# Reordering the statistics, the table terms and the raw products ahead of the first affine step of a pairwise outer-product batch norm

## The chip, the cores and the metric

The kernel runs on one core of a Trainium2 chip. The engines are called as in the profile: PE (matmuls), DVE (vector engine), ACT (scalar engine), POOL (GpSimd) and SP, which issues the stores; the DMA engines move the bytes, and a stretch is called dry where they have little or nothing to move. The metric is the device time of one execution in microseconds (us).

## The reference

```python
cross  = xj[:, rows, :, None] * xi[:, cols, None, :]   # 1024 x 741 x 16 x 16, pairs col < row of 39 fields
mean   = mean(cross, axis=(0, 2, 3)); var = mean((cross - mean)**2, axis=(0, 2, 3))   # one per pair
normed = (cross - mean) * rsqrt(var + 1e-5) * gamma + beta
out    = transpose(normed[:, :, None] * W)             # 777 MB of float32
```

The inputs are 5 MB, the output 777 MB. The mean and the variance of a pair need only sums over the inputs: means and second moments of each field and their products, summed over the batch (a Gram matrix). So the kernel can know scale and shift of every pair before it forms a product, except for the raw products that it forms meanwhile, to have something to do.

## The kernel before

`xi_sb` and `xj_sb` hold the inputs, 128 partitions by 8 slices. The output is cut into tiles of one row of pairs and two slices; `y_sb` has room for four such tiles, and the statistics borrow the place of tiles 2 and 3 in it as scratch. Instructions keep the order of the program on each engine. g1 is the copy of the first Gram product's sums; k, q1 and q2 are terms of the pairs' means and variances (the variance needs q1 less the square of k); "the table" holds scale and shift of every pair. A raw product is one that is not scaled yet; an affine step scales and shifts it. The parts that matter here, shortened ("..." and comments stand for what is left out):

```python
def product(n, engine, t, i, src):          # one of 16 outer-product rows of one slice of tile n
    ...                                      # ACT: activation(Copy, scale=xj);  POOL: tensor_scalar

def affine(n):                               # tiles 0 and 1: scale and shift of raw products, column by column
    for c in range(r):
        if c % 2 == 0: nc.scalar.activation(y[:, :, c], y[:, :, c], Identity, bias=t_c, scale=s_c)   # L194
        else:          nc.gpsimd.tensor_scalar(y[:, :, c], y[:, :, c], s_c, t_c, mult, add)           # L196

def products(n):                             # tiles 2, 3, ...: products of an xi that is scaled already
    split = E - (POOL_I_LONG if tiles[n][0] > TWO else POOL_I)     # rows below split on ACT, 4 of 16 on POOL
    ...
def finish(n):   # DVE (13% of the columns POOL): add the shift, times W, column by column (L238); store the pieces
    ...

# statistics, n = 0..7: xj side for even n, xi side for odd n
for n in range(7): deviation(n)              # POOL, L283
emit(raw0, 3)                                # raw products of tile 0 on ACT
for n in range(8):
    square(n)                                # ACT, L293
    emit(raw0, 2)
    moments(n)                               # DVE, L299
    if n == 0: deviation(7)
    if n % 2 == 1: gram(n // 2 * T)          # PE, L316: 3 products per slice
    if n in (1, 3): sums(n + 3, n + 5); means(n + 3); means(n + 4)      # DVE
emit(raw_products(1, nc.gpsimd, range(8, 32)), 24)      # raw products of tile 1 on POOL
nc.scalar.copy(w_dve, w_sb)
emit(raw0, 8)
nc.scalar.copy(g1, ps_g[0]);  nc.scalar.copy(e_aa, ps_g[1])
emit(raw0, 5)
# table terms, DVE: k, q2, k, q2, p_q1, p_q2, q1, p_mean ... then
nc.scalar.activation(p_kk, k, AF.Square)     # ACT, "the Square"
# DVE: q1, q1 + p_q2, q1 - p_kk, max/eps, reciprocal
nc.scalar.activation(rstd, inv, AF.Sqrt)     # ACT, "the Sqrt"
emit(raw1, 8)                                # raw products of tile 1 on ACT
# DVE: one Newton step, PE: spread over partitions, DVE: table in st_sb
apply(0); affine(0); weigh(0)                # weigh: DVE, times W (L204), and the stores, piece by piece
scale_xi(2); affine(1); weigh(1); apply(2); apply(1)
# then for each tile n: finish(n), products(n + 1)
```

## Time and profile before

| | before |
|---|---|
| median | 1891.21 us (3 runs, 1891.14 to 1891.22) |
| written | 776.99 MB |
| first store | 41.27 us |
| DVE begins tile 2 | 63.96 us |

Lines of the page for groups of instructions give: line, engine, operation, out and in, count, then busy us and mean ns, then the engine's idle time ahead of them and who ended it. These are the affine steps of tiles 0 and 1 in the kernel before:

```profile
L194 ACT ACTIVATE y_sb<-y_sb,st_sb 128x512 f32<-128x512 f32 x20 | 14.2, 797 | 0.0
L196 POOL TENSOR_SCALAR y_sb<-y_sb,st_sb 128x512 f32<-128x512 f32 x18 | 13.5, 771 | 0.3 <-issue 0.3
```

ACT does not idle ahead of them, POOL only 0.3 us. The view in order of time (start and duration in us, then the same columns) shows what fills the place ahead on DVE and POOL:

```profile
23.83 5.52 DVE L299 TENSOR_REDUCE y_sb<-y_sb 128x78 f32<-128x1248 f32 x4
25.86 11.87 POOL L141 TENSOR_SCALAR y_sb<-xi_sb,xj_sb 128x304 f32<-128x304 f32 x24
```

DVE reduces the last moments until 29.35 us. POOL forms its 24 raw products until 37.73, just as the table is ready (37.90).

### The profile page before, as it was taken

The numbers are of one execution on the slowest core, as the hardware profiler recorded it, in microseconds if no ns is written. First come the engines' busy times: TensorE is split into PE (matmuls) and PEld (weight loads), VectorE is DVE, ScalarE is ACT, GpSimd is POOL, SyncE is SP. The second block draws the span as 40 slices with busy tenths as digits, with TensorE's granted clock in tenths as the row PEclk, the third lists the DMA queues.
The fourth block names the chain that finished last, engine by engine and source line by source line (L and its number), as shares of the span: only waits on it lengthen the run. The fifth ranks groups of instructions, "written<-read, shape, count | busy, mean of one in ns | idle before, by whom it ended". The sixth has DMA issues, their size and how long they took to land. (4 is left out here: it accounts for less than half of the span.)

```text
span 1889.3 us, 10288 instructions
## 1 busy us (share of the span) xinstructions
PE 24.5 (1%) x128; PEld 23.1 (1%) x128; DVE 1730.7 (92%) x2612; ACT 1621.3 (86%) x3625; POOL 1574.5 (83%) x1985
## 2 busy tenths in 40 slices
PE   3100000000000000000000000000000000000000
PEld 3100000000000000000000000000000000000000
DVE  7999999998989898989898989899999999999996
ACT  8999989898989898989898989888888888888762
POOL 9798878788888888888888888888888888888972
DMA  4999999999999999999999999999999999999999
GB/s 164 390 418 429 425 427 429 430 424 429 424 425 426 424 424 426 422 425 425 424 425 423 426 423 426 422 422 422 421 421 422 418 415 419 416 419 419 415 419 390
DMA packets 70288, 783.67 MB, mean 415 GB/s; under 512 B 5057, under 2 KB 6209, under 8 KB 15937
## 3 DMA queue, kind: packets, MB, share of 16 engines
q1 hardware_dynamic: 69632, 780.46, 98.3%
q10 hardware_dynamic: 576, 2.56, 0.3%
q14 instruction: 79, 0.64, 0.1%
q8 instruction: 1, 0.02, 0.0%
HBM read 6.00 MB, written 776.99 MB: 414 GB/s over the span
## 5 line engine op out<-in xcount | busy, mean ns | idle before, releaser
L238 DVE SCALAR_TENSOR_TENSOR y_sb<-y_sb,st_sb,w_dve 128x512 f32<-128x512 f32 x2542 | 1678.5, 740 | 131.5 <-issue 128.3
L139 ACT ACTIVATE y_sb<-xs,xj_sb 128x256 f32<-128x256 f32 (+32 forms) x3544 | 1576.4, 539 | 223.5 <-DMA out_dram<-y_sb 171.8
L141 POOL TENSOR_SCALAR y_sb<-xs,xj_sb 128x560 f32<-128x560 f32 (+35 forms) x1256 | 643.2, 536 | 35.1 <-DMA out_dram<-y_sb 32.6
L230 POOL TENSOR_TENSOR y_sb<-y_sb,w_sb 128x1024 f32<-128x1024 f32 (+4 forms) x138 | 442.0, 3203 | 11.5
L159 POOL TENSOR_TENSOR xs<-xi_sb,st_sb 128x576 f32<-128x576 f32 (+37 forms) x150 | 187.8, 1252 | 225.3 <-ACT y_sb L139 217.8
L226 POOL TENSOR_SCALAR y_sb<-y_sb,st_sb 128x512 f32<-128x512 f32 x384 | 259.4, 692 | 12.9 <-ACT y_sb L139 12.9
L204 DVE TENSOR_TENSOR y_sb<-y_sb,w_dve 128x2560 f32<-128x2560 f32 (+5 forms) x8 | 21.0, 2682 | 2.3 <-ACT y_sb L194 2.3
L139 ACT ACTIVATE y_sb<-xi_sb,xj_sb 128x304 f32<-128x304 f32 x40 | 18.7, 534 | 0.1
L414 PE MATMUL ps<-y_sb 39*128 39x38 f32 (+37 forms) x76 | 16.5, 397 | 5.6 <-DVE y_sb L402 5.6
L414 PEld LDWEIGHTS ps<-y_sb 39*128 39x128 f32 x76 | 16.3, 329 | 5.8 <-issue 5.8
L194 ACT ACTIVATE y_sb<-y_sb,st_sb 128x512 f32<-128x512 f32 x20 | 14.2, 797 | 0.0
L196 POOL TENSOR_SCALAR y_sb<-y_sb,st_sb 128x512 f32<-128x512 f32 x18 | 13.5, 771 | 0.3 <-issue 0.3
L141 POOL TENSOR_SCALAR y_sb<-xi_sb,xj_sb 128x304 f32<-128x304 f32 x24 | 11.9, 518 | 0.0
L299 DVE TENSOR_REDUCE y_sb<-y_sb 128x78 f32<-128x1248 f32 x8 | 11.1, 1442 | 0.0
L277 DVE TENSOR_REDUCE y_sb<-xj_sb 128x78 f32<-128x1248 f32 (+1 forms) x5 | 5.9, 1189 | 5.6 <-DMA xj_sb<-in_r_xj_dram 5.6
L293 ACT ACTIVATE y_sb<-y_sb 128x1248 f32<-128x1248 f32 x8 | 9.9, 1243 | 1.3 <-POOL y_sb L283 1.1
L283 POOL TENSOR_TENSOR y_sb<-xj_sb,y_sb 128x1248 f32<-128x1248 f32 x4 | 9.3, 2314 | 1.9 <-ACT y_sb L327 1.9
L283 POOL TENSOR_TENSOR y_sb<-xi_sb,y_sb 128x1248 f32<-128x1248 f32 x4 | 9.3, 2318 | 0.0
L316 PE MATMUL ps<-y_sb 128*39 128x79 f32 x48 | 7.2, 339 | 16.5 <-DVE y_sb L299 16.5
L316 PEld LDWEIGHTS ps<-y_sb 128*39 128x39 f32 x48 | 6.1, 183 | 17.4 <-DVE y_sb L299 9.6
L277 DVE TENSOR_REDUCE y_sb<-xi_sb 128x78 f32<-128x1248 f32 (+1 forms) x5 | 5.9, 1186 | 0.0
L259 POOL TENSOR_SCALAR_AFFINE_SELECT y_sb<-y_sb 39x4992 f32<-39x4992 f32 x1 | 4.6, 4623 | 0.0
(45 smaller groups left out, 16.9 us busy)
## 6 DMA issues: line engine op xcount, KB each, us to landing
out_dram<-y_sb SPq DMA_DIRECT2D x32, 3072.0 KB, 13.7
out_dram<-y_sb SPq DMA_DIRECT2D x28, 2816.0 KB, 15.7
out_dram<-y_sb SPq DMA_DIRECT2D x32, 1664.0 KB, 14.2
out_dram<-y_sb SPq DMA_DIRECT2D x16, 3328.0 KB, 17.2
out_dram<-y_sb SPq DMA_DIRECT2D x30, 1536.0 KB, 15.2
out_dram<-y_sb SPq DMA_DIRECT2D x12, 3840.0 KB, 17.6
out_dram<-y_sb SPq DMA_DIRECT2D x12, 3584.0 KB, 18.1
out_dram<-y_sb SPq DMA_DIRECT2D x22, 1792.0 KB, 17.4
```

The source lines that it names most:

```text
L139: nc.scalar.activation(y, src, AF.Copy, scale=scale)
L141: engine.tensor_scalar(y, src, scale, 1.0, ALU.mult, ALU.mult)
L159: nc.gpsimd.tensor_tensor(xs, xi_sb[:, t0 : t0 + T, 0:r, :], s_sb[:, :, n0 : n0 + r, :].to_broadcast([P, T, r, E]), ALU.mult,)
L194: nc.scalar.activation(y[:, :, c, :], y[:, :, c, :], AF.Identity, bias=t_c, scale=s_c)
L196: nc.gpsimd.tensor_scalar(y[:, :, c, :], y[:, :, c, :], s_c, t_c, ALU.mult, ALU.add)
L204: nc.vector.tensor_tensor(y[:, :, c0:c1, :], y[:, :, c0:c1, :], w_dve.unsqueeze(1).to_broadcast([P, T, c1 - c0, EE]), ALU.mult,)
L226: nc.gpsimd.tensor_scalar(y[:, :, c, :], y[:, :, c, :], t_sb[:, n0 + c : n0 + c + 1], 1.0, ALU.add, ALU.mult)
L230: nc.gpsimd.tensor_tensor(y[:, :, split:r, :], y[:, :, split:r, :], w_sb.unsqueeze(1).to_broadcast([P, T, r - split, EE]), ALU.mult,)
L238: stt(y[:, :, c, :], y[:, :, c, :], t_sb[:, n0 + c : n0 + c + 1], w_dve.to_broadcast([P, T, EE]), ALU.add, ALU.mult,)
L283: nc.gpsimd.tensor_tensor(devs[n % 7], sources[x][:, t0 : t0 + T], shift[:, x : x + 1, :].unsqueeze(3).to_broadcast([P, T, F, E]), ALU.sub ...
L316: nc.tensor.matmul(acc[0:F, 0 : 2 * F + 1], lhs, fb[:, t], start=t == 0, stop=t == NT - 1)
L414: nc.tensor.matmul(ps[:, :, first[r] - n0 : first[r] - n0 + r], pick[:, r, :], stq[:, :, 0:r], start=True, stop=True,)
```

## The change

The statistics take the xi side of each pair of slices first, so that two of the three Gram products can be done while the xj side is still being squared; the last four slices' sums are taken in one batch; g1 is copied as soon as its products are done, and DVE works out the terms of the table that need only g1 beside the last products; four raw products on ACT and six on POOL move from ahead of the first affine step to behind it. The intent is an earlier table and an earlier first store. The diff is shortened:

```diff
 def step_of(n):
-    t0, x = n // 2 * T, n % 2
+    return n // 2 * T, 1 - n % 2                  # xi side first
...
-    for acc, lhs in zip(ps_g, (fa[:, t, 0:F], fa[:, t, F:2*F], ones[:, 0:F])):
+    terms = ((0, fa[:, t, 0:F]), (2, ones[:, 0:F])) if x else ((1, fa[:, t, F:2*F]),)
+    for acc, lhs in terms:
...
-            if n % 2 == 1: gram(n // 2 * T)
-            if n in (1, 3): sums(n + 3, n + 5); means(n + 3); means(n + 4)
+            gram(n)
+            if n == 1: sums(4, 8); means(4, 8)
-        emit(raw_products(1, nc.gpsimd, range(8, 32)), 24)
+        raw1_pool = raw_products(1, nc.gpsimd, range(8, 32))
+        emit(raw1_pool, 18)
         nc.scalar.copy(w_dve, w_sb)
-        emit(raw0, 8)
         nc.scalar.copy(g1, ps_g[0][0:F, 0 : 2 * F + 1])
+        emit(raw0, 3)
         nc.scalar.copy(e_aa, ps_g[1][0:F, 2 * F : 2 * F + 1])
-        emit(raw0, 5)
+        emit(raw0, 10)
...      # DVE: terms of g1 alone first; now q1 - p_kk stands ahead of p_q2 and of q1 + p_q2
         nc.scalar.activation(p_kk, k, AF.Square)
...
         nc.scalar.activation(rstd, inv, AF.Sqrt)
-        emit(raw1, 8)
+        emit(raw1, 4)
...
         apply(0); affine(0)
+        emit(raw1, 4)
+        emit(raw1_pool, 6)
         weigh(0); scale_xi(2); affine(1)
```

More of the change, by code (lines that the diff above doesn't have):

```diff
@@ L279, in sums, with step_of @@
                 )
+        def step_of(n):
+            return n // 2 * T, 1 - n % 2
         def deviation(n):
-            t0, x = n // 2 * T, n % 2
+            t0, x = step_of(n)
             nc.gpsimd.tensor_tensor(
@@ L290, in square, with means, gram @@
         def square(n):
-            scale = 0.25 / NB**0.5 if n % 2 else 0.25
+            _, x = step_of(n)
+            scale = 0.25 / NB**0.5 if x else 0.25
             nc.scalar.activation(devs[n % 7], devs[n % 7], AF.Square, scale=scale)
         def moments(n):
-            t0, x = n // 2 * T, n % 2
+            t0, x = step_of(n)
             to = fb if x else fa
-            at = slice(F, 2 * F)
-            nc.vector.tensor_reduce(to[:, t0 : t0 + T, at], devs[n % 7], AX.X, ALU.add)
-        def means(n):
-            t0, x = n // 2 * T, n % 2
-            to = fb if x else fa
-            stt(
-                to[:, t0 : t0 + T, 0:F],
-                total[:, t0 : t0 + T, part(x)],
-                1.0 / (E * NB) if x else 1.0 / E,
-                ps_u[:, x : x + 1, :].to_broadcast([P, T, F]),
-                ALU.mult,
-                ALU.subtract,
-            )
-        def gram(t0):
+            nc.vector.tensor_reduce(
+                to[:, t0 : t0 + T, F : 2 * F], devs[n % 7], AX.X, ALU.add
+            )
+        def means(t0, t1):
+            for x, to in enumerate((fa, fb)):
+                stt(
+                    to[:, t0:t1, 0:F],
+                    total[:, t0:t1, part(x)],
+                    1.0 / (E * NB) if x else 1.0 / E,
+                    ps_u[:, x : x + 1, :].to_broadcast([P, t1 - t0, F]),
+                    ALU.mult,
+                    ALU.subtract,
+                )
+        def gram(n):
+            t0, x = step_of(n)
             for t in range(t0, t0 + T):
-                for acc, lhs in zip(ps_g, (fa[:, t, 0:F], fa[:, t, F : 2 * F], ones[:, 0:F])):
+                terms = ((0, fa[:, t, 0:F]), (2, ones[:, 0:F])) if x else ((1, fa[:, t, F : 2 * F]),)
+                for acc, lhs in terms:
                     nc.tensor.matmul(
-                        acc[0:F, 0 : 2 * F + 1], lhs, fb[:, t], start=t == 0, stop=t == NT - 1
+                        ps_g[acc][0:F, 0 : 2 * F + 1], lhs, fb[:, t], start=t == 0, stop=t == NT - 1
                     )
@@ L343, in tile_pair_outer_batchnorm @@
         sums(1, 2)
-        means(0)
-        means(1)
+        means(0, 2)
         sums(2, 4)
-        means(2)
-        means(3)
+        means(2, 4)
         for n in range(7):
@@ L355, in tile_pair_outer_batchnorm @@
             moments(n)
+            gram(n)
             if n == 0:
                 deviation(7)
-            if n % 2 == 1:
-                gram(n // 2 * T)
-            if n in (1, 3):
-                sums(n + 3, n + 5)
-                means(n + 3)
-                means(n + 4)
-        emit(raw_products(1, nc.gpsimd, range(8, 32)), 24)
+            if n == 1:
+                sums(4, 8)
+                means(4, 8)
+        raw1_pool = raw_products(1, nc.gpsimd, range(8, 32))
+        emit(raw1_pool, 18)
         nc.scalar.copy(w_dve, w_sb)
-        emit(raw0, 8)
         nc.scalar.copy(g1, ps_g[0][0:F, 0 : 2 * F + 1])
+        emit(raw0, 3)
         nc.scalar.copy(e_aa, ps_g[1][0:F, 2 * F : 2 * F + 1])
-        emit(raw0, 5)
+        emit(raw0, 10)
         e_ab, e_abb, e_a = g1[:, 0:F], g1[:, F : 2 * F], g1[:, 2 * F : 2 * F + 1]
@@ L380, in tile_pair_outer_batchnorm @@
         stt(k, p_b, u, e_ab, ALU.mult, ALU.add)
-        stt(q2, e_ab, u, p_aab, ALU.mult, ALU.add)
+        stt(p_q1, p_bb, u, e_abb, ALU.mult, ALU.add)
         stt(k, p_v, e_a, k, ALU.mult, ALU.add)
-        stt(q2, p_v_half, e_aa, q2, ALU.mult, ALU.add)
-        stt(p_q1, p_bb, u, e_abb, ALU.mult, ALU.add)
-        stt(p_q2, q2, 2.0, p_v, ALU.mult, ALU.mult)
         nc.vector.tensor_add(q1, p_q1, e_abb)
@@ L388, in tile_pair_outer_batchnorm @@
         nc.scalar.activation(p_kk, k, AF.Square)
+        stt(q2, e_ab, u, p_aab, ALU.mult, ALU.add)
         stt(q1, q1, u, p_aabb, ALU.mult, ALU.add)
+        stt(q2, p_v_half, e_aa, q2, ALU.mult, ALU.add)
+        nc.vector.tensor_sub(q1, q1, p_kk)
+        stt(p_q2, q2, 2.0, p_v, ALU.mult, ALU.mult)
         nc.vector.tensor_add(q1, q1, p_q2)
-        nc.vector.tensor_sub(q1, q1, p_kk)
         nc.vector.tensor_scalar(p_var, q1, 0.0, BN_EPS, ALU.max, ALU.add)
```

## The prediction

> **What bounds the kernel now.** I read the page's head, slices and queues first, then the first 85 us in order of time, then the stretches around the first stores.
>
> ```profile
> PE 24.5 (1%) x128; PEld 23.1 (1%) x128; DVE 1730.7 (92%) x2612; ACT 1621.3 (86%) x3625; POOL 1574.5 (83%) x1985
> DMA  4999999999999999999999999999999999999999
> ...
> q1 hardware_dynamic: 69632, 780.46, 98.3%
> ```
>
> No compute engine is the bound over the whole span. The store queue is busy for 98.3% of it and moves 777 MB that the change leaves alone. So the end is "the last moment at which the DMA engines run dry" plus a constant time for the bytes still to come. I looked for that moment in stretches of half a microsecond: DMA share is 0.00 from 70.5 to 72.0 us and 0.07 in 81.5 to 82.0; in every 50 us stretch from 80 us on it is 0.99 to 1.01. So what counts is when the stores at 66.84, 71.31 and 81.31 us (tiles 2 and 3) can be issued, not when the first store leaves. The start in order of time (start, duration, engine, line, what, idle before it):
>
> ```profile
> 28.25 3.61 ACT L139 ACTIVATE y_sb<-xi_sb,xj_sb 128x304 f32<-128x304 f32 x8
> 29.41 1.80 PE L316 MATMUL ps<-y_sb 128*39 128x79 f32 x12 [0.92 <-DVE y_sb L299]
> 31.77 0.20 ACT L372 COPY y_sb<-ps 39x79 f32<-39x79 f32 x1
> 31.92 2.30 ACT L139 ACTIVATE y_sb<-xi_sb,xj_sb 128x304 f32<-128x304 f32 x5
> 32.34 0.24 DVE L382 SCALAR_TENSOR_TENSOR y_sb<-ps,y_sb 39x39 f32<-39x39 f32 x1
> 34.12 0.19 ACT L388 ACTIVATE ps<-y_sb 39x39 f32<-39x39 f32 x1
> 34.35 0.19 DVE L391 TENSOR_TENSOR y_sb<-y_sb,ps 39x39 f32<-39x39 f32 x1 [0.18 <-ACT ps L388]
> 35.23 0.24 ACT L396 ACTIVATE y_sb<-y_sb 39x39 f32<-39x39 f32 x1 [0.91 <-DVE y_sb L395]
> 37.73 0.17 DVE L427 TENSOR_TENSOR st_sb<-ps,st_sb 128x19 f32<-128x19 f32 x1
> 38.06 6.75 POOL L196 TENSOR_SCALAR y_sb<-y_sb,st_sb 128x512 f32<-128x512 f32 x9 [0.34 <-issue]
> 39.13 14.20 ACT L194 ACTIVATE y_sb<-y_sb,st_sb 128x512 f32<-128x512 f32 x20
> 53.23 27.05 ACT L139 ACTIVATE y_sb<-xs,xj_sb 128x304 f32<-128x304 f32 x61
> 63.96 16.55 DVE L238 SCALAR_TENSOR_TENSOR y_sb<-y_sb,st_sb,w_dve 128x512 f32<-128x512 f32 x25 [1.44 <-ACT y_sb L139]
> ```
>
> The reader is to see **ACT as the path of the prologue**: from 28.25 to 63.9 us it idles only 0.91 us (before the Sqrt). It does raw products, the g1 copy, more raw products, the Square of k, the Sqrt, raw products of tile 1, 20 affine steps of tiles 0 and 1 (14.1 us), then 24 products of tile 2 (24 x 0.444 = 10.7 us). DVE waits for the last of them at 63.96 and is then busy without a break to 125 us, so every store from 66.84 on hangs on that moment. L382 finishes k at 32.58, but its Square starts only at 34.12: ACT was still in its five raw products.
>
> **What the Trainium skill says.** "PSUM — Partial Sum Buffer", section "Engine vs sequencer instructions", says the ScalarE, VectorE and GpSimdE queues are strict FIFO. The trace agrees: the late Square just described. "ScalarE: Activation LUTs", section "What ACT_TABLE_LOAD costs", gives 186 ns + 0.833 ns per element, 93 ns more for a pointer operand, and 93 ns overlap; for 304 elements that is 532 ns, 439 from start to start. The trace has 534 and 441. "VectorE: DVE Perf Modes", section "Mode 1× (REGULAR) — the baseline", has one result per cycle; the reduces of 624 and 1248 elements start 0.73 and 1.365 us apart here, about 1.02 ns per element plus 0.09. "HBM Reference", section "Specifications (TRN2)", has a core alone at about 425 GB/s; stretches from 80 us on show 415 to 431, so the store stream has no room left.
>
> **The change, part by part.**
>
> *Statistics on DVE.* DVE has no gap from 9.21 to 29.35, so it sets when the moments end. Two pairs of sums over two slices (4 x 1.365 = 5.46) become two reduces of 2496 elements: with the slope above, an estimate of 2.64 each, 5.28. Four mean steps (0.145 apart, 0.58) become two of 156 columns, an estimate of 0.22 each, 0.44. Saved: 6.04 - 5.72 = 0.3 us. The last moment starts at about 27.6 instead of 27.92, the seventh at 26.25, ending at 27.7. The deviations on POOL (8 x 2.28 us from 7.63, done at 25.87) keep their pace: only the order within pairs turns.
>
> *Matmuls.* The last group shrinks from 12 PE instructions (1.80 us) to 4. PE starts 0.133 apart and one takes 0.338, so an estimate of 0.74: PE ends near 29.8, not 31.21. The sums behind g1 are complete earlier still, after the sixth of eight instructions of the group before: 27.75 + 5 x 0.133 + 0.338 = 28.75.
>
> *ACT before the Square.* Eight raw products used to fill ACT while PE finished. Now g1 comes straight after the copy of w, at 28.25, so ACT stands still until PE is through: 28.8 to 29.1, about 0.65 us lost. Behind it come 3 + 10 raw products where it was 8 + 5: the same 13, still all ahead of the Square. So the Square moves from 34.12 to about 34.8, although k itself is ready some 2 us earlier than before.
>
> *Table terms on DVE.* The terms that the change brings forward end in a wait for that Square: the subtraction now stands before the product for q2 and the addition, which had run during the wait and now run after it. Two instructions at 0.22 us: 0.45 more. So the Sqrt goes from 35.23 to 35.23 + 0.65 + 0.45 = 36.35, and the first table entries (last step 37.73, end 37.90) to about 39.0.
>
> *Affine of tile 0.* ACT used to be held to 39.13 by its eight raw products of tile 1; with four it is free near 38.5 and waits for the table: start about 39.1, no gain. POOL, whose 24 raw products ended at 37.73 and which started at 38.06, now stands idle from 25.87 + 18 x 0.494 = 34.8 to about 39.2. The first store leaves at 41.3 to 41.5, against 41.27.
>
> *The work put behind it.* Four raw products on ACT (4 x 0.441 = 1.76 us) and six on POOL (6 x 0.494 = 2.96) now stand between the affine steps of tiles 0 and 1, and tile 1's affine steps need them all. ACT gets there at 39.1 + 7.05 + 1.76 = 47.9; POOL only at 39.2 + 6.72 + 2.96 = 48.9, and ACT waits for it. Before, ACT started tile 1's affine at 39.13 + 7.05 = 46.18. The shift is 48.95 - 46.18 = 2.77 us. It passes on whole: 10 affine steps, then 24 products, no slack on ACT, so DVE starts tile 2 at about 66.7. POOL's own affine of tile 1 starts near 50.1 (before: 45.99) and ends near 56.9; weighing tile 1 ends near 63.1 instead of 61.18, and 1.4 us of table steps follow. Both lie ahead of 66.7, so neither binds.
>
> **Sum:** 1891.21 + 2.77 = 1893.98, say 1894.0 us.
>
> **Rivals.**
> - *The table comes earlier, as intended, and time falls by 1 to 3 us.* For it: PE ends 1.4 us earlier, POOL has a hole, ACT has four fewer instructions ahead. Against it: the Square's place in ACT's queue. If ACT got to it when k is ready (about 30.2), the Sqrt could be near 32 and affine of tile 0 near 35, giving 1888 to 1890.
> - *Stores hide it.* If what counts were the first store, the time would stay at 1891.2 to 1891.4. For it: the DMA share after 82 us is 1.00. Against it: the dry stretch at 70.5 to 72 wipes out whatever was gained or lost ahead of it.
> - *Only ACT's own work counts*, POOL's six products being ready in time or ACT's g1 wait being shorter: the shift would be 39.1 + 7.05 + 1.76 - 46.18 = 1.7, so 1892.9.
> - *A second wait:* weighing tile 1 on DVE runs over into tile 2 and adds to the shift. It would need 2 us more than I count; 1895 to 1896.
>
> **Range and chances.** All terms are fractions of a microsecond taken from rows of one trace, and three runs before lie within 0.08 us. The main risk is a step of the chain that I misjudge, not scatter. The third rival and some spare give the low end, 1892.2; the fourth and a slower table the high end, 1895.4. I leave one chance in ten for the first two rivals. A change of 2% would be 38 us, as long as the whole time to the first store, so "same" is all but certain.
>
> **What would show it.** Right: the g1 copy at 28.8 to 29.1 with a wait for PE; the Square still behind ten raw products near 34.8, with DVE idle some 3 to 4 us before the subtraction; the Sqrt near 36.3; POOL idle about 4 us before its first affine step near 39.2; ACT idle about 1 us before tile 1's affine, released by POOL; DVE's first step of tile 2 near 66.7; the dry stretch of the DMA moved by the same 2.8 us; the same 0.99 to 1.01 after it. Wrong: a Square near 31 us, an affine of tile 0 before 38 us, or DVE starting tile 2 before 64.5 us while the end moves otherwise.

## More of the kernel before

The view by stretches has, for each stretch of time, the busy us of PE, its weight loads, DVE, ACT and POOL, with counts, then the clock, the share of the DMA engines' time that is busy, and GB/s:

```profile
70.00:72.00 2.00, 0.00 (x0) 0.00 (x0) 2.00 (x4) 2.00 (x6) 2.00 (x6) 1.00 0.16 64
80.00:82.00 2.00, 0.00 (x0) 0.00 (x0) 2.00 (x4) 2.00 (x6) 2.00 (x5) 1.00 0.80 332
100.00:120.00 20.00, 0.00 (x0) 0.00 (x0) 20.00 (x32) 20.00 (x46) 18.42 (x26) 1.00 1.01 420
140.00:142.00 2.00, 0.00 (x0) 0.00 (x0) 1.97 (x6) 2.00 (x5) 1.92 (x3) 1.00 0.75 313
```

The DMA engines are full from about 42 us on, but for dry stretches near 71 and 82 us and short dips such as that at 141.

## The result

The changed kernel takes 1893.85 us (median of 6 runs, 1893.34 to 1894.34), against 1891.22 us for the kernel before (6 runs, 1890.88 to 1891.45). The ratio is 1.0014, 95% interval 1.0001 to 1.0027. By the 2% measure the two are the same; the change costs 2.6 us.

The page of the changed kernel, the affine groups and the store queue (its profile is of the slowest of the six runs, 1894.34 us, so what it shows is about 0.5 us more than a median run has):

```profile
L196 POOL TENSOR_SCALAR y_sb<-y_sb,st_sb 128x512 f32<-128x512 f32 x18 | 13.5, 767 | 4.8 <-ACT y_sb L139 4.8
L194 ACT ACTIVATE y_sb<-y_sb,st_sb 128x512 f32<-128x512 f32 x20 | 14.3, 800 | 1.4 <-POOL y_sb L141 0.9
q1 hardware_dynamic: 69632, 780.46, 98.1%
```

The busy times are as before; what is new is idle time: 4.8 us on POOL, 1.4 us on ACT. The releaser named for POOL's 4.8 us is an ACT raw product that was done at 38.8; what came just ahead of the start was the last table step of DVE (39.05 to 39.22). In order of time:

```profile
28.18 2.11 PE L323 MATMUL ps<-y_sb 128*39 128x79 f32 x12 [0.61 <-DVE y_sb L303]
29.23 0.22 ACT L375 COPY y_sb<-ps 39x79 f32<-39x79 f32 x1 [1.11 <-PE ps L323]
30.71 4.50 ACT L139 ACTIVATE y_sb<-xi_sb,xj_sb 128x304 f32<-128x304 f32 x10
35.11 0.19 ACT L389 ACTIVATE ps<-y_sb 39x39 f32<-39x39 f32 x1
35.34 0.19 DVE L393 TENSOR_TENSOR y_sb<-y_sb,ps 39x39 f32<-39x39 f32 x1 [3.90 <-ACT ps L389]
36.55 0.24 ACT L400 ACTIVATE y_sb<-y_sb 39x39 f32<-39x39 f32 x1 [1.25 <-DVE y_sb L399]
39.30 7.17 ACT L194 ACTIVATE y_sb<-y_sb,st_sb 128x512 f32<-128x512 f32 x10 [0.51 <-ACT y_sb L139]
46.11 2.98 POOL L141 TENSOR_SCALAR y_sb<-xi_sb,xj_sb 128x304 f32<-128x304 f32 x6
49.13 7.16 ACT L194 ACTIVATE y_sb<-y_sb,st_sb 128x512 f32<-128x512 f32 x10 [0.91 <-POOL y_sb L141]
66.93 3.38 DVE L238 SCALAR_TENSOR_TENSOR y_sb<-y_sb,st_sb,w_dve 128x512 f32<-128x512 f32 x5 [2.60 <-ACT y_sb L139]
```

ACT waits 1.11 us for PE. Then ten raw products stand ahead of the Square, for which DVE waits 3.90 us. ACT waits 1.25 us for the reciprocal, 0.51 us for the table, and 0.91 us for POOL's six late products. In sum ACT idles 3.78 us between 28 and 67 us, against 0.91 us before; the difference, 2.87, is all but the 2.97 us by which DVE begins tile 2 later (66.93 against 63.96). The first store leaves at 41.46, only 0.19 us later. The dry stretches have moved and grown:

```profile
68.00:70.00 2.00, 0.00 (x0) 0.00 (x0) 2.00 (x4) 2.00 (x6) 1.92 (x4) 1.00 0.42 172
74.00:76.00 2.00, 0.00 (x0) 0.00 (x0) 2.00 (x4) 2.00 (x6) 1.95 (x4) 1.00 0.44 183
84.00:86.00 2.00, 0.00 (x0) 0.00 (x0) 2.00 (x4) 2.00 (x6) 2.00 (x5) 1.00 0.78 323
```

The last one stands at 84.5 instead of 81.5 us, 3 us later. The bytes written up to 80 us, summed from the stretches, are 13.1 MB instead of 14.3 MB, and this gap of 1.2 MB, which is 2.9 us at 420 GB/s, is still there at 600 us.

### The profile page after: what moved, and what is told of

It reads as the page before. It is cut to its first block, busy times and chain, and to the rows that moved or that the text cites. A ratio compares the mean times of both kernels' runs of the same rounds, so it can differ in the third digit from the quotient of the medians.

```text
span 1892.6 us, 10284 instructions
## 1 busy us (share of the span) xinstructions
PE 25.4 (1%) x128; PEld 22.8 (1%) x128; DVE 1730.5 (91%) x2608; ACT 1621.6 (86%) x3625; POOL 1574.5 (83%) x1985
## 5 line engine op out<-in xcount | busy, mean ns | idle before, releaser
L194 ACT ACTIVATE y_sb<-y_sb,st_sb 128x512 f32<-128x512 f32 x20 | 14.3, 800 | 1.4 <-POOL y_sb L141 0.9
L277 DVE TENSOR_REDUCE y_sb<-xj_sb 128x39 f32<-128x624 f32 (+2 forms) x4 | 5.8, 1454 | 6.1 <-DMA xj_sb<-in_r_xj_dram 6.1
L277 DVE TENSOR_REDUCE y_sb<-xi_sb 128x39 f32<-128x624 f32 (+2 forms) x4 | 5.8, 1443 | 0.0
## 6 DMA issues: line engine op xcount, KB each, us to landing
out_dram<-y_sb SPq DMA_DIRECT2D x32, 1664.0 KB, 14.3
```

Source lines behind the costliest of these rows:

```text
L194: nc.scalar.activation(y[:, :, c, :], y[:, :, c, :], AF.Identity, bias=t_c, scale=s_c)
```

## The experiments

Each kernel ran five times, in rounds with the kernel before on the same chip, whose median was 1891.15 to 1891.29 in all of them. All gave correct results. The changed kernel itself was not run again in these rounds; its row is from the result above. The table has for each what the theories are about: when DVE begins tile 2 and when the first store leaves (in the profiled run), and the median.

| run | DVE begins tile 2 | first store | median (range) |
|---|---|---|---|
| before | 63.96 | 41.27 | 1891.22 |
| changed | 66.93 | 41.46 | 1893.85 (1893.34 to 1894.34) |
| a_pool_back | 65.56 | 40.91 | 1893.23 (1892.94 to 1893.35) |
| b_g1_filled | 65.76 | 40.29 | 1893.07 (1892.86 to 1893.27) |
| h_terms_back | 66.39 | 40.93 | 1893.61 (1893.33 to 1893.78) |
| d_early_square | 65.12 | 39.64 | 1892.38 (1892.32 to 1892.48) |
| c_early_table | 64.12 | 39.45 | 1891.48 (1891.10 to 1891.74) |
| e_late_store | 63.74 | 44.06 | 1891.26 (1890.79 to 1891.38) |
| g_pool_share | 62.37 | 41.20 | 1889.70 (1889.57 to 1889.87) |
| k_order_share | 60.68 | 37.34 | 1888.13 (1887.87 to 1888.40) |
| f_fine_pieces | 63.88 | 41.20 | 1890.96 (1890.76 to 1891.06) |
| j_fine_all | 63.81 | 41.13 | 1891.12 (1890.97 to 1891.25) |
| l_combined | 60.60 | 37.26 | 1888.03 (1887.91 to 1888.44) |
| m_cut_on | 60.77 | 37.43 | 1888.20 (1887.92 to 1888.35) |

The theory: the time moves one for one with the moment at which DVE begins tile 2, which ACT sets. The rivals: the first store sets it; the early table is worth having for itself; the store stream's dry stretches set it. Over the first ten rows the median moves by 5.7 us and the DVE column by 6.25 us, in the same order but for two pairs that lie 0.2 us apart (a and b, e and before). The first store does not order them: d and c send it 1.6 and 1.8 us earlier than before and are not faster than before, e sends it 2.8 us later and is not slower.

The medians and the profiled runs are not the same executions. For the profiled runs alone, the time less the DVE column lies between 1827.05 and 1827.68 us in all fourteen rows. The traces show how the moment is carried on: in each of them DVE works for 197.9 us from its first step of tile 2 without a wait (198.3 in j and l, with one wait of 0.3), up to about 260 us. Just ahead of that ACT waits 4.5 to 4.6 us for a store to land, and only this wait reaches DVE, which then stands about 4 us.

### a_pool_back: the six POOL products back in front

```diff
-emit(raw1_pool, 18)
+emit(raw1_pool, 24)
 ...
-emit(raw1_pool, 6)
```

> The changed kernel with all 24 raw products of tile 1 on POOL put back ahead of the first affine step; the four on ACT stay behind it. My theory (the path runs through the affine steps of tile 1, which ACT may begin only when POOL's six late products are done): POOL does the six in its 4.8 us hole, ACT begins the affine of tile 1 near 48.2 instead of 49.13 with no wait for POOL, DVE begins tile 2 near 66.0 instead of 66.93, time down by 0.9 us against the changed kernel, to about 1892.9. Rival (only ACT's own count of work and the late table matter; POOL's part is hidden): time unchanged at 1893.8.

Measured: 1893.23 us. The second half of the affine steps no longer waits for POOL:

```profile
38.74 7.16 ACT L194 ACTIVATE y_sb<-y_sb,st_sb 128x512 f32<-128x512 f32 x10 [0.51 <-ACT y_sb L139]
47.75 7.16 ACT L194 ACTIVATE y_sb<-y_sb,st_sb 128x512 f32<-128x512 f32 x10
```

From the first to the second line it is 9.01 us instead of 9.83 in the changed kernel, so 0.82 us of the expected 0.9 came from POOL's products. The rest of the 1.37 us in the DVE column was there from the start: g1 came at 28.67 instead of 29.23 in this profile, with the same program up to there, because the loads had landed sooner.

### b_g1_filled: ACT works while PE finishes

```diff
 nc.scalar.copy(w_dve, w_sb)
+emit(raw0, 8)
 nc.scalar.copy(g1, ...)
-emit(raw0, 3)
 nc.scalar.copy(e_aa, ...)
-emit(raw0, 10)
+emit(raw0, 5)
```

> The changed kernel with eight of the thirteen raw products of tile 0 put back ahead of the copy of g1, as before the change. My theory (ACT's 1.11 us wait for PE ahead of g1 is lost for good, since ACT is the path): the Square comes near 34.0 instead of 35.11, DVE begins tile 2 near 65.8, time down by 1.1 us to about 1892.7, although the terms on DVE start 2 us later. Rival (the early g1 is worth having, because the terms are then done beside the last matmuls): time up by 0.5 us or more.

Measured: 1893.07 us; g1 comes with no wait, the Square at 33.95 instead of 35.11, DVE in tile 2 at 65.76, 1.17 us earlier:

```profile
31.59 0.20 ACT L376 COPY y_sb<-ps 39x79 f32<-39x79 f32 x1
33.95 0.19 ACT L389 ACTIVATE ps<-y_sb 39x39 f32<-39x39 f32 x1
```

In the medians the gain is 0.78 us. So the terms begin 2.4 us later and the end comes earlier. The terms done beside the last matmuls were worth nothing, because what they end in waits for the Square.

### h_terms_back: the old order of the terms

```diff
-k, p_q1, k, q1, p_mean | q2, q1, q2, q1 - p_kk, p_q2, q1 + p_q2, max
+k, q2, k, q2, p_q1, p_q2, q1, p_mean | q1, q1 + p_q2, q1 - p_kk, max
```

> The changed kernel with the DVE instructions of the table terms in their old order, so that only the maximum with the added epsilon follows the subtraction. My theory (two DVE instructions now stand behind the wait for the Square): the step from the subtraction to the reciprocal shrinks from 0.78 to 0.45 us, Sqrt 0.33 us earlier, DVE begins tile 2 0.33 us earlier, near 66.6, time down by 0.3 us to about 1893.5. Rival (order does not matter because something else is waited for): unchanged, DVE begins tile 2 at 66.9.

Measured: 1893.61 us. The time alone does not tell (the ranges overlap with the changed kernel's); the trace does: from the Square to the Sqrt it is 1.11 us (34.91 to 36.02) instead of 1.44 (35.11 to 36.55), the 0.33 expected. The other 0.2 us of the DVE column is g1's arrival again (29.03 against 29.23).

### d_early_square: the Square ahead of the ten products

```diff
-nc.scalar.copy(e_aa, ...)
-emit(raw0, 10)
 ... # k is ready
 nc.scalar.activation(p_kk, k, AF.Square)
+nc.scalar.copy(e_aa, ...)
+emit(raw0, 10)
```

> The changed kernel with the Square and the copy of e_aa put behind three raw products, ahead of the other ten; the Sqrt stays behind the ten. My theory (the Sqrt then takes over the place of the Square as what waits for the ten raw products): DVE has the reciprocal ready near 32.5, the Sqrt comes near 35.4 instead of 36.55, DVE begins tile 2 near 65.8, time down by 1.1 us to about 1892.7. Rival (the Square's place is the whole cause): time back to 1891.2 or below.

Measured: 1892.38 us. The Square came at 30.18, and yet the Sqrt only at 34.74, with no wait of ACT ahead of it: the ten products now stand ahead of the Sqrt.

```profile
30.18 0.19 ACT L387 ACTIVATE ps<-y_sb 39x39 f32<-39x39 f32 x1
34.74 0.23 ACT L400 ACTIVATE y_sb<-y_sb 39x39 f32<-39x39 f32 x1
```

The gain is 1.5 us in the medians and 1.81 us in the DVE column; of the latter, 0.50 is g1's earlier arrival in this profile (28.73 against 29.23).

### c_early_table: the table as early as it can be

```diff
+# Square and e_aa behind 3 raw products, then
+emit(raw0, 3)
 nc.scalar.activation(rstd, inv, AF.Sqrt)
+emit(raw0, 7)
 emit(raw1, 4)
```

> The changed kernel with the Square put right behind the first three raw products and the Sqrt behind three more, the other seven behind the Sqrt: what the change seems to have meant. My theory (ACT's work up to the products of tile 2 is conserved; an earlier table cannot make ACT faster, only take idle time away): Sqrt near 32.5, table about 35.2, but ACT is through with tile 0's raw products only near 36, affine of tile 0 near 37.8, DVE begins tile 2 near 64.3, time about 1891.6, so no gain over the kernel before. Rival (of my prediction: a table 3 to 4 us earlier is worth 1 to 3 us): 1888 to 1890.

Measured: 1891.48 us, within 0.3 us of the kernel before. ACT in order of time:

```profile
32.34 0.23 ACT L400 ACTIVATE y_sb<-y_sb 39x39 f32<-39x39 f32 x1 [0.44 <-DVE y_sb L399]
32.48 4.92 ACT L139 ACTIVATE y_sb<-xi_sb,xj_sb 128x304 f32<-128x304 f32 x11
46.31 7.16 ACT L194 ACTIVATE y_sb<-y_sb,st_sb 128x512 f32<-128x512 f32 x10
```

The Sqrt is 4.2 us earlier than in the changed kernel and 2.9 us earlier than before. But the raw products that had stood ahead of it now stand behind it, and ACT begins tile 1's affine at 46.31, where the kernel before has it at about 46.18 (39.13 + 10 x 0.705). An early table by itself buys nothing here: ACT has the same work to do up to tile 2, and only its waits can be taken away.

### e_late_store: the first store 2.8 us later

```diff
-(0, 2, 5, 9, 14, 19)
+(0, 5, 9, 14, 19)
```

on the kernel before.

> The kernel before with the first two pieces of tile 0 joined, so that the first store leaves about 1.9 us later (near 43.2 instead of 41.27) and nothing else moves on the compute engines. My theory (the DMA engines run dry at 70.3 to 72.1 us in any case, which swallows a later start of up to that much): time unchanged within 0.4 us, 1891.2, and the dry stretch shorter. Rival (store stream is the bound from the first store on): time up by 1.9 us to 1893.1.

Measured: 1891.26 us, unchanged, although the first store left at 44.06 us, later than I had meant. The dry stretch took it up:

```profile
70.00:72.00 2.00, 0.00 (x0) 0.00 (x0) 2.00 (x4) 2.00 (x6) 2.00 (x5) 1.00 0.94 370
```

where the kernel before has 0.16. What is lost or won at the first store is gone by 75 us.

### g_pool_share: less work for ACT in tile 2

```diff
-split = E - (POOL_I_LONG if tiles[n][0] > TWO else POOL_I)
+split = E - (6 if n == 2 else POOL_I_LONG if tiles[n][0] > TWO else POOL_I)
```

on the kernel before.

> The kernel before with six instead of four of the sixteen products per slice of tile 2 on POOL, which stands idle for 6 us there. Nothing of the table or of the statistics changes. My theory (ACT's way to the last product of tile 2 sets the end): ACT is through 1.8 us earlier, near 62.1; DVE is busy with table steps until 62.5 and begins tile 2 there instead of 63.96; time down by 1.4 us to about 1889.8. Rival (the first store or the table sets the end): unchanged at 1891.2.

Measured: 1889.70 us, no overlap with the kernel before (1890.69 to 1891.58 in these rounds). DVE goes into tile 2 at 62.37 straight from its table steps, without a wait for ACT. A lever that touches neither statistics nor table moves the end as the theory says.

### f_fine_pieces and j_fine_all: filling the dry stretches by smaller stores

```diff
-(0, 4, 11, 19), (0, 9, 19), (0, 10, 20), (0, 9, 18), (0, 10, 20), (0, 9, 18)                  # tiles 2 to 7
+(0, 3, 6, 9, 13, 19), (0, 4, 9, 14, 19), ...                                                     # f: tiles 2, 3
+(0, 3, 6, 9, 13, 19), (0, 4, 9, 14, 19), (0, 5, 10, 15, 20), (0, 5, 9, 18), (0, 5, 10, 20), (0, 5, 9, 18)   # j
```

on the kernel before.

> The kernel before with the stores of tile 2 cut into five pieces (0,3,6,9,13,19) instead of three and those of tile 3 into four (0,4,9,14,19) instead of two. No engine's compute changes. My theory (the end is the last dry moment of the DMA engines plus a constant): the dry stretches of 1.8 us at 70.3 and of 0.7 us at 81.5 shrink to well under half, DVE still begins tile 2 at 64.0, time down by 1 to 2 us to about 1889.7. Rival (dry stretches do not matter, or smaller stores cost as much as they win): 1891.2 or more.

> The kernel before with finer stores for all of tiles 2 to 7, not for tiles 2 and 3 alone. In the run with tiles 2 and 3 alone the dry stretches at 70.3 and 81.5 us were gone, but a new one of about 1.7 us stood at 90 to 94 us, where tile 4's first store still waits for ten of its columns. My theory (the end is the last dry moment plus a constant): with tile 4 to 7 cut as well no stretch below half share is left after 67 us; the dry 2.3 us are saved, of which smaller stores give back about 1 us (395 to 410 GB/s over some 50 us instead of about 415); time about 1889.9. Rival (something else than dry stretches sets the end): 1891.0 as with two tiles cut.

Measured: 1890.96 and 1891.12 us. Both expectations failed. The stretches near 71 and 82 us were indeed full (share 1.02), and j had written 0.7 MB more than the kernel before by 100 us. The lead then went, as j's stretches show:

```profile
70.00:72.00 2.00, 0.00 (x0) 0.00 (x0) 2.00 (x4) 2.00 (x6) 2.00 (x5) 1.00 1.02 393
100.00:120.00 20.00, 0.00 (x0) 0.00 (x0) 20.00 (x32) 20.00 (x47) 18.41 (x26) 1.00 1.02 412
140.00:142.00 2.00, 0.00 (x0) 0.00 (x0) 1.97 (x6) 2.00 (x6) 1.92 (x2) 1.00 0.34 139
```

In 100 to 120 us j's full engines move 412 GB/s, those of the kernel before 420, and at 141 us, ahead of the first store that was left whole, the engines ran dry. In f the same happened in 90 to 94 us (share 0.57), and at 140 to 142 us again (0.63).

### k_order_share, l_combined, m_cut_on: a version that beats both

k takes the changed kernel's order of statistics and PE work, gives ACT raw products at each point where it had waited, and takes the larger POOL share in tile 2:

```diff
 nc.scalar.copy(w_dve, w_sb)
+emit(raw0, 2)
 nc.scalar.copy(g1, ...);  emit(raw0, 3);  nc.scalar.copy(e_aa, ...)
-emit(raw0, 10)
 nc.scalar.activation(p_kk, k, AF.Square)
+emit(raw0, 4)
 nc.scalar.activation(rstd, inv, AF.Sqrt)
-emit(raw1, 4)
+emit(raw0, 4); emit(raw1, 1)
 ... affine(0)
-emit(raw1, 4)
+emit(raw1, 7)
-split = E - (POOL_I_LONG ...)
+split = E - (7 if n == 2 else POOL_I_LONG ...)
```

> A version meant to beat both: the changed kernel's statistics and PE order, but ACT given raw products at every point where it waited (two ahead of g1, four between Square and Sqrt, five behind the Sqrt, seven of tile 1's behind the affine of tile 0), and seven instead of four of sixteen products per slice of tile 2 on POOL. Theory: table near 35.0, affine of tile 0 on ACT near 35.2, affine of tile 1 near 45.4, DVE begins tile 2 near 60.5 instead of 63.96; time down by 3.4 us against the kernel before, to about 1887.8. Rival (store stream or DVE's weighing becomes the bound earlier): gain under 2 us.

Measured: 1888.13 us, 3.1 us below the kernel before and 5.7 below the changed one; ratio to before 0.9984, interval 0.9971 to 0.9996. ACT's path in order of time:

```profile
32.42 0.23 ACT L401 ACTIVATE y_sb<-y_sb 39x39 f32<-39x39 f32 x1
35.17 7.16 ACT L194 ACTIVATE y_sb<-y_sb,st_sb 128x512 f32<-128x512 f32 x10 [0.32 <-ACT y_sb L139]
45.51 7.16 ACT L194 ACTIVATE y_sb<-y_sb,st_sb 128x512 f32<-128x512 f32 x10
```

One wait of 0.32 us is left of 3.78. Tile 1's affine begins at 45.51, 0.7 us earlier than before; the remaining 2.6 of the 3.28 us in the DVE column come from POOL's share (18 instead of 24 products on ACT).

l adds finer stores for tiles 1 to 7, m also cuts those of tiles 8 to 15 in two:

> The version with ACT's waits filled and POOL's larger share, and finer stores for tiles 1 to 7. Theory: first store near 37.3, no dry stretch of the DMA engines of over half a microsecond after 40 us, so the end becomes the first store plus all bytes: 1885.5, within 1884.5 to 1887. Rival (smaller stores cost as much as the dry stretches): 1887.8, as without them.

> The combined version with the stores of tiles 8 to 15 cut in two as well. In the runs with finer stores up to tile 7 the bytes written were 0.5 to 0.8 MB ahead until 120 to 140 us and the lead was lost at one spot: the store of the first uncut tile (issued at 141.09 us with the kernel before, at 138.26 in the combined version), ahead of which the DMA engines ran dry for 1.4 to 2.2 us. Theory (the end is the last dry moment plus a constant): with the next eight tiles cut no stretch under half share is left between 45 and 180 us, the lead of about 0.7 MB stays, time down by 1 to 1.8 us against 1888.0, to about 1886.6. Rival (DVE's unbroken chain up to 260 us and not the dry DMA sets the end, or smaller stores are slower by as much): 1888.0 again.

Measured: 1888.03 and 1888.20 us; both gains failed to come. In l the engines still ran dry ahead of the first store left whole (share 0.62 in 138 to 140 us). In m no stretch is dry any more after 68 us, so the dry stretches are not what is left to gain. Its lead over k in bytes written was 0.44 MB at 120 and 0.46 at 160 us, 0.14 at 200 and gone by 250. In 160 to 200 us, where m still stores in halves, k's line comes first and then m's, one in each fence:

```profile
160.00:200.00 40.00, 0.00 (x0) 0.00 (x0) 40.00 (x62) 36.58 (x84) 33.12 (x42) 1.00 1.01 429
```

```profile
160.00:200.00 40.00, 0.00 (x0) 0.00 (x0) 40.00 (x62) 38.66 (x89) 36.68 (x48) 1.00 1.01 421
```

The engines are equally full, and 8 GB/s over 40 us are the 0.32 MB lost. This is more than scatter: the thirteen other kernels, which store these tiles whole, show 425 to 432 GB/s in the same 40 us. So m's smaller stores gave back what they had won; why they run slower is not settled by these runs. Nor is m's other rival, DVE's unbroken chain, excluded: that chain is as long in m as in k (197.9 us), and m's time is the 1888 that this rival foretold.

That f and j come out like the kernel before, and l like k, has a plainer reading in the traces, though no run tests it: the last dry stretch had not moved. The kernel before already runs short at 141 us (share 0.75, shown above), 77 us after DVE begins tile 2, ahead of the first store left whole; f and j run dry at the same place, l, like k, 77 us after its own start, near 138 us.

## Why the prediction was right

The time, 1893.85, lies 0.15 us from the 1894.0 predicted. So close a hit is partly luck: g1 alone moves by 0.56 us between profiles of one beginning (below), and errors of both signs cancelled. The mechanism is what was right. By its own steps:

- **What counts is when DVE can begin tile 2.** Right. The prediction put it at 66.7; it was 66.93. Seven variants and two kernels follow it, and with the profiled runs' own times all fourteen do; e shows that the first store does not count.
- **Statistics on DVE, 0.3 us saved.** Right as a count of work, incomplete as a time. The estimates for the larger instructions held (the 2496-element reduces were 2.67 us apart against 2.64 estimated, the two wide mean steps took 0.45 together). But I left out the loads. In the profile of the changed kernel DVE waited 1.11 us for the third load (0.71 before) and 0.22 us for the last, which the batch needs whole, and the last moment's reduce ended at 29.48 instead of 29.35: nothing saved. In that of a_pool_back, the same program up to there, the waits were 0.72 and none, and it ended at 28.93: 0.4 us saved.
- **ACT's wait ahead of g1, 0.65 us.** The term that was mis-sized most: 1.11 in the profile of the changed kernel, 0.45 to 0.83 in the four other profiles with the same beginning (h, d, c, a). ACT got to g1 at 28.12, 0.13 us earlier than reckoned; the rest is g1 coming at 29.23 instead of 28.8 to 29.1, and the cause of that is the same. In the five profiles (changed, h, c, d, a) the last six reduces of the moments begin at 21.24, 21.04, 20.87, 20.75 and 20.68 us and g1 is copied at 29.23, 29.03, 28.86, 28.73 and 28.67: always 7.98 to 7.99 us later, so how soon the loads land passes whole into g1. It will be a part of the changed kernel's larger scatter between runs; no run shows how large a part. Runs b and k, which fill the wait, show that it was on the path.
- **The Square behind all thirteen products.** Right: 35.11 against 34.8, 0.3 us later because g1 was. DVE idle 3.90 us, as foretold.
- **Two DVE instructions behind the Square, 0.45 us.** Right in kind; h measured 0.33.
- **No gain at the affine of tile 0.** Right: 39.30 on ACT (39.1 predicted), 39.38 on POOL (39.2), POOL idle 4.81 us.
- **ACT waits for POOL's six late products.** Right: 0.91 us of wait (about 1 predicted), affine of tile 1 at 49.13 (48.95); a took the wait away and got 0.82 us.
- **The sum.** 2.77 predicted, 2.97 in the profile (of a run of 1894.34, the slowest of six), 2.63 in the medians. What the profile has too much is the Square's 0.3 us, partly offset by the DVE steps, 0.33 instead of 0.45. Two sums of the prediction are rounded up: 35.23 + 0.65 + 0.45 is 36.33, and POOL's 39.2 + 6.72 + 2.96 is 48.88; with 48.88 the shift would be 2.70.

Two things around the prediction fell. The first rival said that a table 3 to 4 us earlier would give 1888 to 1890; c made that table and got 1891.48, because ACT's work up to tile 2 stays the same wherever the table falls. And the picture of "last dry moment plus a constant" was too simple. It took 81.5 to 82 us for the last dry moment and overlooked the one at 141 us. Where only the compute moved it gave the right shift, since the stores hang on DVE's unbroken work. f, j and l filled only the earlier dry stretches; m, which filled the last one too, won nothing either.

The intent of the change failed at one point: the Square and the Sqrt sit in the queue of the engine that has the most to do there. Bringing their inputs forward without moving them made DVE wait longer, and the work taken from ahead of the affine steps came back behind them, when POOL had no hole left.

The Trainium skill, "Perfetto Trace Analysis", section "Optimization Strategy", says that the most-contended engine can change between regimes of one kernel. The runs agree: over the span it is the store queue (98.3%), but the 5.7 us between the changed kernel and k were decided in the first 67 us, on the path that runs through ACT.

## What to carry to other kernels

Ask first at which moment the engines' lead over the bound resource is decided, and which engine sets it; there, an order is worth just the idle time that it takes away or adds on that engine. An instruction that others wait for must be moved forward in its own queue, not only its inputs, and a filler product belongs where its engine would otherwise wait, neither earlier nor later. A gain at the first store or in a dry stretch of the queue is worth nothing until it is seen at the end.

## What the Trainium skill lacked or had wrong

- "DMA: Bandwidth & Descriptors", section "Measured (HBM→SBUF, 128 partitions, SWDGE, issued from GpSimd)", has single loads by size (1 MB at 341 GB/s). It lacks stores that follow one another in a full queue: there, j's stores of 0.8 to 2.6 MB ran at 393 GB/s (70 to 72 us) and 412 GB/s (100 to 120 us), and m, which halves the stores of whole tiles, shows 421 GB/s in 160 to 200 us, where the thirteen kernels that do not halve them show 425 to 432.
- None of the pages that I read says how far the landing of one and the same load differs between executions: DVE's wait for the third load was 0.72 to 1.11 us, and for the last one none or 0.22 us, in five profiles with the same beginning, and the copy of g1 moved by 0.56 us with it.
